# Two reorderings in a fused residual kernel: when the first chunk's part stores go out, and when the last weight rows are prepared

## The chip, the cores and the metric

The kernel runs on one core of one Trainium2 chip. The metric is the device time of one execution in microseconds. Before the change it is 2336.32 us, the median of 3 runs (2335.76 to 2338.26). The execution that was profiled took 2337.22 us.

## The reference

The input `x` has 32 sequences of 64 rows and 1024 columns in float32. Four layers are added to it in turn; each reads what the one before left:

```
x = x + causal_convolution(x, state-space parameters) * length_mask
x = x + einsum('bsi,boi->bso', x, W1[id1[b]])         # 16 matrices of 1024 x 1024
x = x + einsum('bij,bkj->bik', x, W2[id2[b]])         # 16 matrices of 1024 x 1024
gate = x @ W_gate.T + 0.5 * low_rank(A_gate, B_gate, id3[b])   # 2752 hidden units
up   = x @ W_up.T   + 0.5 * low_rank(A_up, B_up, id3[b])
act  = silu(gate) * up
x = x + act @ W_down.T + 0.5 * low_rank(A_down, B_down, id3[b])
```

The matrix of the second and third layer and the low-rank pair of the fourth are picked for each sequence.

## The kernel before

The 32 sequences are worked through in four chunks of 8, that is 512 rows each. The convolution is done for all at the start (about the first 200 us). Then the adapters of chunk 0 run. After that a loop over the chunks runs the gated layer, and the adapters of the next chunk are slotted into it, one at a time (`other()`, called by `between`): an adapter is 128 matmuls on TensorE (L297) over eight weight tiles of 512 KB, `wa`, which SyncE's queue loads (L167).

**The gated layer.** The 2752 hidden units are ten pairs of 128-row blocks and a rest. `gated` makes two such pairs a call, once for the gate and once for the up half; I call one of these a step, so chunk 0 has ten steps (five groups, `g` 0 and 1). All products are done by the scheme of Strassen and Winograd, which needs seven block products in place of eight, but wants sums and differences of the weight blocks. `sides` makes four of them on VectorE (L453 to L456).

- In chunk 0 (`halves`) the scheme is applied once. Each step has two units `m` = 0 and 1 of seven products (L540). While it holds the weights, it also makes and stores to DRAM what the later chunks will want: `kept(q)` makes a second level of sums in one of two `kept` buffers and stores it to `sums` (L517), and `kept_parts` stores some raw blocks and first-level sums to `parts` (L527 and L530). All these stores are issued by GpSimd (POOL).
- In the chunks 1 to 3 (`quarters`) the scheme is applied twice and the stored `sums` and `parts` are loaded.

In a step the sums come in the order `kept(0)`, `kept(1)` (unit 0), `kept(2)`, `kept(3)` (unit 1). The third needs the buffer of the first, so VectorE's L453 in it waits until the first store has landed. Behind it VectorE has L572 and L574, which read PSUM banks that TensorE's sixth product of the unit writes again. `kept_parts` is called just before `kept(2)`, but a store goes out when POOL's queue reaches it: POOL and SyncE are ordered by the planner, while TensorE, VectorE and ScalarE follow the program's order. `kept_parts` makes four stores a step: for `wts[0][1]` (256 KB) and `sts[0]` (768 KB), which are ready before unit 0, and for `wts[1][1]` (128 KB) and `sts[1]` (384 KB), ready during it.

The loaded weight tiles (`wf`, `wd`, `wa` and others) share nine rotating 512 KB buffers of `wpool`. A load into a buffer waits in SyncE's queue until all that read it is done, stores from it included, and all later loads wait behind it.

**The down product.** At the end of each of three blocks of hidden units, `ffn` multiplies the activations with `W_down` (L1018): for each of four `h`, over slices `s0` of the block, seven products `j`. In the last block there are two slices. With the second slice of each `h`, the tail products `po<-rest,wl` are added: `wl` holds the gathered low-rank rows (two gathers, POOL, L326) and the last 64 rows of `W_down`; `rest2` is their moving operand. `wl` needs a copy of 64 partitions on ScalarE (L1007) and one subtraction on VectorE (L1008). Only the tail of the last product, `j` = 2, reads the difference. `rest2` is written by `low_rank_down` on VectorE: a multiply (L410), an add (L412) and four copies (L416).

After the first slice the program calls `down_sides` (four `sides` operations for weights to come) and, at `h` = 0, `low_rank_down`.

Of the kernel before, what the change touches and what calls it, by code (L numbers as in the profile page):

```python
# [41 lines left out]
TQ, KQ = TH // 2, KH // 2  # L42
QP = KQ * P
# [30 lines left out]
def kernel(  # L74
# [25 lines left out]
    nc = tc.nc  # L100
# [12 lines left out]
    def ps_tile(name):  # L113
        return psum.tile([P, 512], F32, tag="ps", name=name)
# [266 lines left out]
    FIRST, SECOND = slice(0, P // 2), slice(P // 2, P)  # L381
# [115 lines left out]
    def halves(c, gi, g, o, xb, sides0, early, also=lambda: None):  # L497

        name = f"{c}_{gi}_{g}"
        lt, copy_lt = low_rank_of(c, gi, g)  # L500
        wts, sts, sides_of = ([x] for x in sides0)

        def kept(q):

            src = [
                [wts[m][0] for m in range(MG)],
                [wts[m][1] for m in range(MG)],
                [sts[m][:, 0:2] for m in range(MG)],
                [sts[m][:, 2:3] for m in range(MG)],
            ][q]  # L510
            n = 1 if q == 3 else 2
            t = qpool[0].tile([P, 2, 4, KQ, P], F32, tag="kept", name=f"kept{q}_{name}", bufs=2)
            a11, a12, a21, a22 = (
                src[m][:, :, k * KQ : (k + 1) * KQ, :] for m in range(MG) for k in range(2)
            )
            sides(a11, a12, a21, a22, *(t[:, :n, i] for i in range(4)))
            nc.gpsimd.dma_start(  # L517
                sums[2 * gi + g][2 * q : 2 * q + n].rearrange("j p e -> p j e"),
                t[:, :n].rearrange("p j i k f -> p j (i k f)"),
            )  # L520

        def kept_parts():

            d = parts[2 * gi + g]
            for lo, n, at_ in ((0, 1, [wts[m][1][:, 0:1] for m in range(MG)]), (1, 3, sts)):
                to = d[lo : lo + n].rearrange("j p e -> p j e")
                nc.gpsimd.dma_start(  # L527
                    to[:, :, : 2 * QP], at_[0][:, :n].rearrange("p j k f -> p j (k f)")
                )
                nc.gpsimd.dma_start(  # L530
                    to[:, :, 2 * QP :],
                    at_[1][:, :n, KQ:].rearrange("p j k f -> p j (k f)"),
                )

        for m in range(MG):
            ws = sides_of[m]

            def product(ps, j, start):
                for kt in range(KH):
                    nc.tensor.matmul(  # L540
                        ps,
                        ws[j][:, kt, :],
                        xb[j][:, kt, :],
                        start=start and kt == 0,
                        stop=kt == KH - 1,
                        skip_group_check=True,
                    )


            pa, pb, pc = (ps_tile(f"pf{i}_{name}_{m}")[:, :TH] for i in range(3))  # L550
            c11, c12, c21, c22 = (
                o[:, i, m, t * TH : (t + 1) * TH] for i in (0, 1) for t in (0, 1)
            )
            u, v = (
                gpool.tile([P, 2 * TQ], F32, tag=f"u{i}", name=f"u{i}_{name}_{m}", bufs=1)
                for i in range(2)
            )
            product(pa, 0, True)
            nc.scalar.copy(u, pa)
            product(pb, 5, True)  # L560
            nc.scalar.copy(v, pb)
            nc.vector.tensor_add(u, v, u)
            if m == 0:
                copy_lt()
                for at_, x in zip((wts, sts, sides_of), halves_sides(gi, g, 1)):
                    at_.append(x)
                also()
            else:
                kept_parts()
                kept(2)  # L570
            product(pc, 6, True)
            nc.vector.tensor_add(c22, pc, u)  # L572
            product(pb, 4, True)
            nc.vector.tensor_add(c22, pb, c22)  # L574
            kept(3 * m)
            product(pa, 1, False)
            nc.scalar.copy(c11, pa)
            product(pb, 2, False)
            nc.vector.tensor_add(c12, pb, u)
            if m == 0:  # L580
                kept(1)
            else:
                early()
            product(pc, 3, False)
            nc.vector.tensor_add(c21, pc, u)
            o_m = o[:, :, m]
            nc.vector.tensor_add(o_m, o_m, lt[:, :, m])
        if g == 0 or (gi + 1) * MG not in [m1 for _, m1 in BLOCKS]:
            return halves_sides(gi + g, 1 - g, 0)
# [274 lines left out]
    def ffn(c, xb, sides0, others):  # L864
# [40 lines left out]
        for block, (m0, m1) in enumerate(BLOCKS):  # L905
            last = m1 == FM
# [4 lines left out]
            def down_sides(done=False):  # L911
                nonlocal sides0
                if not todo:
                    if c == 0 and not last and sides0 is None and (done or block == 0):
                        sides0 = halves_sides(m1 // MG, 0, 0)
                    return
                h, s0 = todo.popleft()
                name = f"{c}_{block}_{h}_{s0}"
                wt = wpool.tile([P, 2, 2, SEG, P], F32, tag="w", name=f"wd_{name}")
                nc.sync.dma_start(  # L920
                    wt.rearrange("p i k s f -> p (i k s f)"), wd[h, s0 // SEG]
                )
                st = gpool.tile([P, 3, SEG, P], F32, tag="s", name=f"s_{name}")
                down[h, s0] = stationary([wt[:, 0], wt[:, 1]], SEG, st)
# [11 lines left out]
            for gi in groups:  # L936
                end = gi == groups[-1]
# [27 lines left out]
            if block == 0:  # L965

                wl = gpool.tile([P, KH, 3, P], F32, tag="cu", name=f"wm_{c}", bufs=1)
# [10 lines left out]
            if last:  # L978


                wl = gpool.tile([P, 2, 2, L // 2], F32, tag="lt", name=f"wl_{c}", bufs=1)
# [8 lines left out]
            for h in range(KH):  # L990
# [7 lines left out]
                for s0 in range(m0, m1, SEG):  # L998
                    end = s0 + SEG == m1
                    ws = down.pop((h, s0))  # L1000
                    tails = {}
                    if block == 0:
                        w = [wl[:, h, i] for i in range(3)]
                        tails = {1: (w[0], 0), 3: (w[1], 0), 4: (w[1], 1), 2: (w[2], 1)}
                    elif end and last:
                        if h == 0:
                            nc.scalar.copy(wl[SECOND, 1], wl[SECOND, 0])  # L1007
                            nc.vector.tensor_sub(wl[:, 1, 0], wl[:, 1, 0], wl[:, 1, 1])  # L1008
                        w = [[wl[:, t, i, h * P : (h + 1) * P] for i in (0, 1)] for t in (0, 1)]
                        tails = {1: (w[0][0], 0), 3: (w[0][1], 0), 4: (w[1][1], 1), 2: (w[1][0], 1)}  # L1010
                    for j in (0, 5, 6, 4, 1, 3, 2):
                        terms = [(ws[j][:, i, :], ab[s0 - m0 + i][j]) for i in range(SEG)]
                        if j in tails:
                            w, t = tails[j]
                            a = rest2[:, t] if last else rest1[:, t * TH : (t + 1) * TH]
                            terms.insert(SEG if s0 == m0 else 0, (w, a))
                        for i, term in enumerate(terms):
                            nc.tensor.matmul(  # L1018
                                pss[j],
                                *term,  # L1020
                                start=(s0 == m0 and i == 0 and home[j] % 2 == 0),
                                stop=(end and i == len(terms) - 1),
                                skip_group_check=True,
                            )
                    down_sides(h == KH - 1 and end)
                    if s0 == m0 and block == 1 and h < KH - 1:
                        other()
                    if h == 0 and s0 == m0:
                        tv = low_rank_down(at, ins, f"d{block}_{c}", tv, last)
                    if h == 1 and s0 == m0 and not last:  # L1030
                        at = next_at()
                    if s0 == m0 and last and h and more_come:

                        if h < KH - 1:
                            ready = raw.popleft()()
                        if h == 1:
                            raw.append(columns(au, c + 1, KT, f"u_{c + 1}"))
                        steps[h]()
# [497 lines left out]
```

## Time and profile before

| | us |
|---|---|
| median of 3 runs | 2336.32 |
| profiled execution | 2337.22 |
| its span, first to last instruction | 2335.6 |
| TensorE matmul, busy | 2256.3 (97%) |
| VectorE, busy | 1319.6 (57%) |
| ScalarE, busy | 379.7 (16%) |
| GpSimd, busy | 268.7 (12%) |
| moved by DMA | 684.96 MB, of it 82.37 MB in GpSimd's queue |

The granted TensorE clock was 0.998 over the span. The stretches that the change touches lie in this execution at about 349 to 840 us (the steps of chunk 0) and about 840 to 850, 1360 to 1370, 1880 to 1890 and 2280 to 2290 us (the first `h` of the last down product of each chunk). Share of busy time alone says little here, since TensorE is busy nearly throughout: what counts is where TensorE stands still, and for whom.

### The profile page before, as it was taken

To read this page: it belongs to the slowest core of one execution; us is meant where nothing else is said; L and a number is where in the kernel's file an instruction comes from. 1 tells how busy PE (TensorE), PEld (TensorE's weight loads), DVE (VectorE), ACT (ScalarE), POOL (GpSimd) and SP (SyncE) were. 2 spreads that over 40 slices of the span, in tenths; PEclk is the share of its full clock that TensorE was granted. 3 is DMA by queue.
4 is the path that set the end of the run, shared out by engine and by line. 5 is a ranking of instruction groups with operands and counts; after the bars stand their busy time and mean duration, and the time that the engine had idled before them with its cause. 6 is when DMAs were issued, how large, how long until landed. Compare 5 with 4: busy or idle time off the path is not lost.

```text
span 2335.6 us, 53669 instructions
## 1 busy us (share of the span) xinstructions
PE 2256.3 (97%) x21674; PEld 1863.4 (80%) x21674; DVE 1319.6 (57%) x2792; ACT 379.7 (16%) x822; POOL 268.7 (12%) x387
## 2 busy tenths in 40 slices
PE   5999889999999999999999999999999999999999
PEld 4996437677768789678768889688769889799997
DVE  7411116657636676646534677646535676577585
ACT  4200002010101112112102212112102212121220
POOL 3323002211101121000000011000000011100000
PEclk9999999999999999999999999999999999999999
DMA  8989998779997956889997956889997947285581
GB/s 293 366 314 361 407 409 304 279 293 345 357 365 290 348 202 209 309 291 344 366 349 291 359 188 229 308 297 360 358 347 284 359 159 266 95 292 204 193 278 62
DMA packets 201802, 684.96 MB, mean 293 GB/s; under 512 B 26178, under 2 KB 28482, under 8 KB 201042
## 3 DMA queue, kind: packets, MB, share of 16 engines
q1 hardware_dynamic: 169570, 590.50, 69.2%
q0 software_dynamic: 25184, 82.37, 9.4%
q10 hardware_dynamic: 6800, 8.65, 1.0%
q8 instruction: 171, 2.80, 0.5%
q14 instruction: 77, 0.63, 0.1%
HBM read 614.02 MB, written 67.40 MB: 292 GB/s over the span
## 4 chain that ended last, share of the span: by engine, by line
PE 77%; DMA 14%; issue 5%; DVE 3%; POOL 1%; ACT 0%; SPq 0%; POOLq 0%; ACTq 0%; DVEq 0%
PE pq L631 28%; PE po L1018 22%; PE pa L297 11%; DMA wa<-in_w 8%; PE pc L1324 5%; PE pr L764 4%; PE pf L540 3%; DMA sums<-kept 2%; PE pe L427 2%; DMA hk<-kp 1%; PE pl_d L398 1%; DMA wf<-in_wg 1%; DMA wa<-sums 1%; POOL parts L530 0%; DVE br L1126 0%
## 5 line engine op out<-in xcount | busy, mean ns | idle before, releaser
L297 PE MATMUL pa<-wa,x 128*32 128x256 f32 x7872 | 457.6, 381 | 26.2 <-DMA wa<-in_w 24.1
L297 PEld LDWEIGHTS pa<-wa,x 128*32 128x32 f32 x7872 | 243.0, 110 | 225.8 <-DMA wa<-in_w 63.8
L631 PE MATMUL pq<-xd,wa 128*128 128x128 f32 x3360 | 415.3, 275 | 0.3 <-DMA wa<-sums 0.2
L631 PEld LDWEIGHTS pq<-xd,wa 128*128 128x128 f32 x3360 | 394.8, 192 | 0.9 <-DMA wa<-sums 0.7
L631 PE MATMUL pq<-xd,wb 128*128 128x128 f32 x2520 | 323.9, 276 | 0.0
L631 PEld LDWEIGHTS pq<-xd,wb 128*128 128x128 f32 x2520 | 300.6, 192 | 3.8 <-DMA wb<-parts 0.2
L307 DVE STREAM_TRANSPOSE y<-pa 128x512 f32<-128x512 f32 x64 | 45.9, 717 | 291.8 <-PE pa L297 291.8
L1324 PE MATMUL pc<-uf,hk 128*128 128x256 f32 (+7 forms) x1024 | 156.4, 315 | 12.7 <-DMA hk<-kp 8.1
L1018 PE MATMUL po<-act,wd 128*128 128x256 f32 x640 | 168.6, 386 | 0.0
L1324 PEld LDWEIGHTS pc<-uf,hk 128*128 128x128 f32 x1024 | 150.8, 197 | 17.6 <-issue 11.7
L1018 PE MATMUL po<-actd,wd 128*128 128x256 f32 x640 | 164.2, 379 | 0.0
L1018 PE MATMUL po<-actd,s 128*128 128x256 f32 x640 | 164.2, 379 | 0.0
L326 POOL DMA_INDIRECT bgu<-in_bgu,rows x44 | 52.0, 1181 | 925.4 <-PE pe L427 822.1
L540 PE MATMUL pf<-xd,wf 128*128 128x256 f32 x640 | 150.6, 381 | 0.0
L1018 PEld LDWEIGHTS po<-act,wd 128*128 128x128 f32 x640 | 117.8, 190 | 30.0 <-issue 14.6
L453 DVE TENSOR_TENSOR s<-wd 128x256 f32<-128x256 f32 x80 | 33.9, 423 | 188.1 <-PE po L1018 188.0
L1018 PEld LDWEIGHTS po<-actd,wd 128*128 128x128 f32 x640 | 121.6, 190 | 16.5
L1018 PEld LDWEIGHTS po<-actd,s 128*128 128x128 f32 x640 | 121.6, 190 | 16.5
L540 PEld LDWEIGHTS pf<-xd,wf 128*128 128x128 f32 x640 | 120.9, 190 | 17.3
L540 PE MATMUL pf<-xd,s 128*128 128x256 f32 x480 | 116.1, 385 | 7.4 <-DVE up L574 3.6
L1046 ACT COPY uo<-po 128x256 f32<-128x256 f32 x48 | 17.9, 372 | 629.2 <-PE po L1018 627.1
L540 PEld LDWEIGHTS pf<-xd,s 128*128 128x128 f32 x480 | 91.4, 192 | 23.8 <-DVE up L574 5.5
(227 smaller groups left out, 2551.7 us busy)
## 6 DMA issues: line engine op xcount, KB each, us to landing
wa<-in_w SPq DMA_DIRECT2D x492, 512.0 KB, 7.3
wa<-sums SPq DMA_DIRECT2D x210, 512.0 KB, 5.9
wb<-parts SPq DMA_DIRECT2D x120, 384.0 KB, 5.4
wd<-in_wd SPq DMA_DIRECT2D x80, 512.0 KB, 7.0
wb<-in_wq SPq DMA_DIRECT2D x90, 384.0 KB, 5.7
hk<-kp SPq DMA_DIRECT2D x30, 1024.0 KB, 8.6
sums<-kept POOLq DMA_DIRECT2D x30, 1024.0 KB, 7.1
wf<-in_wg SPq DMA_DIRECT2D x20, 512.0 KB, 6.6
```

The costliest lines, as they stand in the source:

```text
L297: nc.tensor.matmul(acc[i * S : (i + 1) * S, s * 256 : (s + 1) * 256], xs[c][:, kt, lo + s * S : lo + (s + 1) * S], wt[:, i * 256 : (i + 1) ...
L307: nc.vector.transpose(y, acc)
L326: nc.gpsimd.indirect_dma_start(out=t, out_offset=None, in_=table, in_offset=bass.IndirectOffsetOnAxis(ap=at_, axis=0),)
L398: nc.tensor.matmul(ps[pair(j)], at[:, i, pair(j)], x_i[:, 2 * H * j : 2 * H * (j + 1)], start=(i == 0), stop=(i == n - 1),)
L427: nc.tensor.matmul(ps[:, at_ * 2 * H : (at_ + 1) * 2 * H], bt[pair(j), g], tms[table][pair(j)], start=(g == 0), stop=True, skip_group_chec ...
L453: nc.vector.tensor_add(s1, a21, a22)
L540: nc.tensor.matmul(ps, ws[j][:, kt, :], xb[j][:, kt, :], start=start and kt == 0, stop=kt == KH - 1, skip_group_check=True,)
L631: nc.tensor.matmul(ps[:, to * TQ : (to + 1) * TQ], w[i][:, k, :], xb[:, j, SLOT[i], k, :], start=start and k == 0 and to == 0, stop=k == K ...
L764: nc.tensor.matmul(ps, wts[i][:, kt, :], xs[c][:, kt, :], start=(kt == 0), stop=(kt == KT - 1),)
L1018: nc.tensor.matmul(pss[j], *term, start=(s0 == m0 and i == 0 and home[j] % 2 == 0), stop=(end and i == len(terms) - 1), skip_group_check=True,
L1046: nc.scalar.copy(u1, p1)
L1324: nc.tensor.matmul(ps[:, j, d * B :], hk[:, j, d * P : (d + 1) * P], uf[:, i + j, : KT - d, :].rearrange("p k b -> p (k b)"), start=(d == ...
```

## The change

It has two parts. In the first chunk, `kept_parts` ties its four stores behind the last store that `kept` made before it, that of `kept(1)`. In every chunk, the copy and the subtraction on `wl` move from the beginning of the second slice of `h` = 0 to the end of the first slice's products, ahead of `down_sides` and `low_rank_down`.

```diff
+        last_kept = []
         def kept(q):
...
-            nc.gpsimd.dma_start(
+            stored = nc.gpsimd.dma_start(
                 sums[2 * gi + g][2 * q : 2 * q + n].rearrange("j p e -> p j e"),
                 t[:, :n].rearrange("p j i k f -> p j (i k f)"),
             )
+            last_kept[:] = [stored.ins]
 
         def kept_parts():
 
             d = parts[2 * gi + g]
             for lo, n, at_ in ((0, 1, [wts[m][1][:, 0:1] for m in range(MG)]), (1, 3, sts)):
                 to = d[lo : lo + n].rearrange("j p e -> p j e")
-                nc.gpsimd.dma_start(
-                    to[:, :, : 2 * QP], at_[0][:, :n].rearrange("p j k f -> p j (k f)")
-                )
-                nc.gpsimd.dma_start(
-                    to[:, :, 2 * QP :],
-                    at_[1][:, :n, KQ:].rearrange("p j k f -> p j (k f)"),
-                )
+                with tc.issue_after(last_kept[0]):
+                    nc.gpsimd.dma_start(
+                        to[:, :, : 2 * QP],
+                        at_[0][:, :n].rearrange("p j k f -> p j (k f)"),
+                    )
+                    nc.gpsimd.dma_start(
+                        to[:, :, 2 * QP :],
+                        at_[1][:, :n, KQ:].rearrange("p j k f -> p j (k f)"),
+                    )
...
                     elif end and last:
-                        if h == 0:
-                            nc.scalar.copy(wl[SECOND, 1], wl[SECOND, 0])
-                            nc.vector.tensor_sub(wl[:, 1, 0], wl[:, 1, 0], wl[:, 1, 1])
...
+                    if last and h == 0 and not end:
+                        nc.scalar.copy(wl[SECOND, 1], wl[SECOND, 0])
+                        nc.vector.tensor_sub(wl[:, 1, 0], wl[:, 1, 0], wl[:, 1, 1])
                     down_sides(h == KH - 1 and end)
```

`issue_after` on the same queue is an order alone, with no semaphore. The program order that results: on TensorE and ScalarE nothing moves. On VectorE the subtraction stands eight instructions earlier in each chunk, behind the `sides` for the second slice of `h` = 0 and ahead of those for the first slice of `h` = 1. On POOL each step's order becomes gather of `bgu`, store of `kept(0)`, of `kept(1)`, the four stores of parts (first the two of `wts[m][1]`, then the two of `sts`), store of `kept(2)`, of `kept(3)`; before, the parts of unit 0 stood ahead of the gather and those of unit 1 behind it, ahead of `kept(0)`. On SyncE the order of the loads is the same.

## The prediction

> **What bounds the kernel now.** I read the page's busy times and its chain first: TensorE is the bound, and the chain leaves it only for transfers and a little VectorE work.
>
> ```profile
> PE 2256.3 (97%) x21674; PEld 1863.4 (80%) x21674; DVE 1319.6 (57%) x2792; ACT 379.7 (16%) x822; POOL 268.7 (12%) x387
> PE 77%; DMA 14%; issue 5%; DVE 3%; POOL 1%; ACT 0%; SPq 0%; POOLq 0%; ACTq 0%; DVEq 0%
> ```
>
> So an edit is worth what it does to TensorE's idle time. Second, who TensorE waited for from 339 to 875 us, the steps of chunk 0 (total, times, longest):
>
> ```profile
> PE pf L540 <- DVE up L574: 3.6, 3, 2.7
> PE pf L540 <- DVE act L574: 3.2, 2, 2.1
> PE pa L297 <- DMA wa<-in_w: 2.3, 6, 0.7
> PE po L1018 <- ACT at_g L373: 1.0, 1, 1.0
> ```
>
> The first two rows, 6.8 us together, are what the first edit can win. L574 is late because `kept(2)` ahead of it waits for a store; VectorE's waits in the same stretch have
>
> ```profile
> DVE kept L453 <- DMA sums<-kept: 21.6, 18, 3.4
> ```
>
> Third, one step in time, on POOL (start, duration, what), and the chain's row for the first of its `sums` stores (start, duration):
>
> ```profile
> 488.08 0.57 POOL L530 DMA_DIRECT2D parts<-wf  x1 [5.35 <-DVE wf L455]
> 488.68 0.76 POOL L530 DMA_DIRECT2D parts<-s  x1
> 492.08 0.73 POOL L517 DMA_DIRECT2D sums<-kept  x1 [2.63 <-DVE kept L456]
> 495.19 0.72 POOL L517 DMA_DIRECT2D sums<-kept  x1 [2.38 <-DVE kept L456]
> ```
> ```profile
> 492.08 6.75 DMA sums<-kept
> ```
>
> Half a megabyte of parts goes out less than 4 us ahead of the store on which VectorE will wait. Fourth, the second edit's place in chunk 0, VectorE and then TensorE:
>
> ```profile
> 843.10 0.42 DVE L456 TENSOR_TENSOR s<-wd,s 128x256 f32<-128x256 f32 x1
> 843.43 0.42 DVE L453 TENSOR_TENSOR s<-wd 128x256 f32<-128x256 f32 x1
> ...
> 845.62 0.91 DVE L416 COPY rest<-tv_d 32x128 f32<-32x128 f32 x4
> 846.55 0.69 DVE L1008 TENSOR_TENSOR wl<-wl 128x512 f32<-128x512 f32 x1
> ```
> ```profile
> 846.62 0.67 PE L1018 MATMUL po<-rest,wl 128*128 128x256 f32 x2 [1.05 <-ACT at_g L373]
> ```
>
> VectorE runs without a gap here, and TensorE stands still 1.05 us until the last copy of `rest` ends (845.62 + 0.91 = 846.53). The row names ScalarE, but its `wl` copy was over at 842.1; what ends last is L416. The other chunks show the same with idle times of 0.70, 0.69 and 0.69 us (at 1366.63, 1885.25, 2284.59).
>
> **Second edit: a loss.** The subtraction moves to between the two rows at 843.10 and 843.43. Where it stood, it cost nothing: the product that reads it, `j` = 2, starts its tail at 850.58, 3.3 us after it ended. In its new place it lies ahead of the copies that TensorE waits for, in a queue with no slack. Two independent 128x512 operations of VectorE start 0.60 us apart (L455 at 487.10, L456 at 487.70), so L416 ends 0.6 us later and TensorE waits 0.6 us more: 4 chunks x 0.6 = 2.4 us.
>
> It also meets a new wait: for the second gather of `wl`. That gather is issued at 839.11, 1353.58, 1872.20 and 2271.55 us and takes 5.0, 9.7, 9.6 and 10.3 us to land, that is 844.1, 1363.3, 1881.8 and 2281.8. The new slots are at 843.4, 1363.4, 1882.1 and 2281.4. So chunk 0 waits 0.7 us and chunk 3 0.4 us, with TensorE behind them. Bounds: nothing, if the gathers land a little earlier, to some 4 us, if those of chunk 0 fall behind the parts' bytes and the others take the longest landing. I take 1.1, the rows as they stand. Queued behind the waiting subtraction are the `sides` for the next `h`, L410, L412 and L416. Second edit: +2.4 + 1.1 = +3.5 us. The copy on ScalarE keeps its place and costs nothing.
>
> **First edit: what it can win.** A step's parts are 256 + 128 + 768 + 384 KB = 1.57 MB. POOL's queue moved 82.37 MB in 9.4% of the 16 engines' span, 0.375 MB/us when it runs. So the 0.52 MB of unit 1, less than 4 us ahead of `kept(0)`, are worth up to 1.4 us of its landing, and all four up to 4.2 us where loads still crowd the engines. TensorE's stalls behind L574 are, step by step, 2.69 (at 404.32), 0.13, 0.56, 1.12, 0.34, 0.09, 0.10 and 2.13 us (at 798.51). Six are below 1.4. At 786.25 the store of `kept(0)` took 8.69 us behind loads issued up to 774.4 that landed as late as 788.7, with 1.57 MB of parts among them; 2.13 us is less than what they took. At 404.32 POOL itself was late: `kept(0)` was ready at 391.2, but issued at 393.30, behind both pairs of parts; that order goes, and with it about 1.5 of the 2.69 us. I count the whole 6.8 us. Bounds: 6.8, and about 3 if half of the crowding is other loads. A rule of the Trainium skill, page "DMA: Bandwidth & Descriptors", section "Anatomy of one DMA — SWDGE (gpsimd) path", gives a transfer from GpSimd about 2.0 us and its bytes at 436 GB/s: an estimate of 4.4 us for `kept(0)`, where the trace has 6.75. By the rule 2.3 us a step could be won; by the rows 1.4. Both cover the six small stalls, so the sum is the same by either.
>
> **First edit: what it adds.** Four stores of 0.57, 0.57, 0.76 and 0.76 us move behind `kept(1)` on POOL: 495.2 + 0.7 + 2.7 = 498.6, before `kept(2)` is ready (501.5), so issuing costs nothing. But the reads of the weight buffers end later, and two who wait for that stand on the way.
>
> First, SyncE. In seven steps an adapter follows, and the loads of its `wa` 5 and 7 (counted from 0) go into the buffers that the two `wts[m][1]` held:
>
> ```profile
> 495.02 11.45 SPq L167 DMA_DIRECT2D wa<-in_w  x3
> ```
>
> These are `wa` 5 at 495.02, 6 at 502.28 and 7 at 506.14. Before, 5 went as soon as `kept(1)` had read the buffer. Now it waits until the part's store has landed, behind `kept(0)` and `kept(1)` in POOL's queue: `kept(1)` landed at 503.0; with less ahead of it I put it at 501.5, plus 0.39 MB at 0.375, so 502.5. Queued behind 5 are 6, 7 and all later loads. TensorE's adapter begins at 506.04 and uses a tile each 0.88 us: 5 at 510.4, 6 at 511.3, 7 at 512.2. Issued at 502.5 with the 5.8 us that `wa` 5 took among stores, it lands at 508.3. 6 follows it about 2 us later, at 510.3. 7 is issued, as before, when TensorE frees its buffer at 506.1, and before took 5.6 us (511.7), 0.5 us ahead of its use. Now two loads stand in front of it and 1.5 MB of `kept(2)` and `kept(3)`, pushed back by 1.15 MB of `sts`, run beside it. I estimate 6.5 us, 0.4 late: 7 x 0.4 = 2.8 us. Bounds: nothing, and 7 x 2.1 = 15 us, if each of the three loads moves at half of 0.375 MB/us (2.7 us each, from 503.5). The same page, section "Queues, rings and completion order", says that each engine takes turns between queues packet by packet, so the stores pushed back do not yield to the loads. By half of its 436 GB/s three loads from 503.5 and 2 us of fixed time end at 512.7, 0.5 us late: 3.5 us in place of 2.8, the sum +0.2 rather than -0.5.
>
> Second, VectorE writes `s` of unit 0 again for the next step (507.82), and now the store of `sts[0]` must have landed. It follows `kept(1)` with 1.18 MB in 3.1 us: 504.6 by the time above, 3 us ahead. Where no adapter lies between, after the first step, `kept(1)` landed at 376.40: 379.5 against 380.85. I count nothing; the bound is 2 us. The loads in the first two steps that also wait for these buffers (`cv`, `wr`, `wd`) are used 10 us or more later.
>
> **Sum.** -6.8 + 2.8 + 3.5 = -0.5 us on the profiled execution's 2337.22 us. That one stands 0.9 us above the median, which it leaves alone: 2336.32 - 0.5 = 2335.8 us.
>
> **Rivals.**
> - *The held buffers turn into a new wait* (slower). Once the loads of `wa` 5 to 7 come so late that the last lands more than 6.2 us after the adapter's first matmul, each of seven adapters pays. At 1.5 to 2.1 us each: -6.8 + (10.5 to 14.7) + 3.5, which is 2343.5 to 2347.7 us. From 0.47 us each on the change is a loss, from 1.15 us each on one of over 0.2%. For it: margins of 0 to 0.9 us in landings of 5.3 to 6.3 us. Against: 5 and 6 have 4 us between the part's landing and the adapter.
> - *The stalls go and nothing takes their place* (faster): the gathers in time, the loads as before: -6.8 + 2.4 = -4.4 us. The crowd of prefetches meets no parts, so that some of the 2.3 us of waits for `wa` go too: 2330.5 to 2331.9. For it: in the long run of loads after each adapter landings take 10 to 13 us beside the parts.
> - *The first half does not do what it says*: `kept(0)` is slowed by loads, not by parts, so `kept(2)` waits as before. Then 0 to -2, with up to 2.8, and +3.5: 2338 to 2340.6.
>
> **How the numbers follow.** My forecast 0.40, the third rival 0.14, the new wait 0.31, the faster one 0.15. A difference of 0.2% (4.7 us) is about what a measurement of this kernel can tell from no change. The first and third lie within it: with a small tail of theirs moved to slower, same 0.52, slower 0.33, faster 0.15. The forecast's own range is 2332 to 2340. The range for 8 in 10 leaves out the upper half of the slower rival and part of the faster one: 2331 to 2344.
>
> **What would show it.** Right: TensorE's waits on L574 fall from 6.8 us to under 1; the idle time before the first `po<-rest,wl` grows to about 2.4, 1.3, 1.3 and 1.7 us, with L1008 ahead of L410; SyncE's `wa` 5 is issued some 7 us later in each step; waits of `pa` for `wa` grow from 2.3 to about 5 us in chunk 0. Wrong: waits on `wa` beyond 10 us in chunk 0, or VectorE waiting at `s` L453 for the store of `sts[0]` with TensorE behind it; or L574's row unchanged.

## The result, and the profile after

The changed kernel takes 2357.48 us (median of 6 runs, 2350.36 to 2359.96); the kernel before, run beside it, 2336.04. The ratio is 1.0089, with a 95% interval of 1.0065 to 1.0113: about 21 us slower, where 2335.8 was predicted and 2344 was the upper end of the range. The profiled execution took 2359.26 us, its span is 2357.6. Lines have moved: L540 is now L545, L574 is L579, L517 is L519, L527 and L530 are L531 and L535, L1018 is L1020, L1008 is L1029.

The page's busy times say that no work was added; TensorE's share fell by a point. (That it is busy 5.5 us longer fits the half-clock stretches told of below.)

```profile
PE 2261.8 (96%) x21674; PEld 1861.9 (79%) x21674; DVE 1319.6 (56%) x2792; ACT 379.7 (16%) x822; POOL 267.9 (11%) x387
```

Who TensorE waited for in chunk 0, 339 to 900 us (total, times, longest):

```profile
PE pa L297 <- DMA wa<-in_w: 13.5, 12, 2.2
PE po L1020 <- DVE rest L416: 6.4, 1, 6.4
PE pf L545 <- DVE up L579: 1.4, 2, 0.9
PE pf L545 <- DVE act L579: 0.9, 1, 0.9
```

The stalls that the first edit was to win shrank from 6.8 to 2.3 us, so it does what it says. The waits for `wa` grew from 2.3 to 13.5, and the one ahead of the tail products from 1.05 to 6.4. VectorE in the same stretch: the waits of L453 for stores of `kept` fell from 21.6 us (18 times, ahead of `kept(2)` and of `kept(3)`) to 9.0 (9 times, all ahead of `kept(2)`), and a new wait is there.

```profile
DVE kept L453 <- DMA sums<-kept: 9.0, 9, 1.6
DVE wl L1029 <- DMA wl<-in_bd,rows_half: 4.7, 1, 4.7
```

One step on POOL (start, duration): both `kept` stores of unit 0 now go ahead of the four parts.

```profile
484.15 0.72 POOL L519 DMA_DIRECT2D sums<-kept  x1 [9.37 <-DVE kept L456]
487.26 0.73 POOL L519 DMA_DIRECT2D sums<-kept  x1 [2.38 <-DVE kept L456]
487.99 0.57 POOL L531 DMA_DIRECT2D parts<-wf  x1
...
489.86 0.77 POOL L535 DMA_DIRECT2D parts<-s  x1
493.80 0.72 POOL L519 DMA_DIRECT2D sums<-kept  x1 [3.17 <-DVE kept L456]
```

What that does to `wa` is best seen at the step whose adapter has the longest wait. SyncE's three loads `wa` 5 to 7, of before and then of after (start of the first issue, time to the end of the last):

```profile
595.18 11.66 SPq L167 DMA_DIRECT2D wa<-in_w  x3
```
```profile
599.59 4.31 SPq L167 DMA_DIRECT2D wa<-in_w  x3
```

The adapter begins at 606.41 us before and at 603.47 after. So the first load went out 11.2 us ahead of it, and now goes 3.9 us ahead; the other two keep about their places (the second 4.0 us ahead before and 3.3 after, the third 0.1 us behind the adapter's start in both), so that all three now go out within 4.3 us. TensorE in the changed kernel:

```profile
603.47 6.25 PE L297 MATMUL pa<-wa,x 128*32 128x256 f32 x112
611.95 1.24 PE L297 MATMUL pa<-wa,x 128*32 128x256 f32 x16 [2.23 <-DMA wa<-in_w]
```

Seven of the eight tiles run without a gap, and the last, `wa` 7, is 2.23 us late. Its row also shows a loss that is no wait: 16 matmuls take 1.24 us, where the other tiles take 0.89, since a stretch at half clock begins just after the stall. Windows of 3.41 us around it (stretch, its length, TensorE busy, granted clock, DMA share, GB/s):

```profile
609.31:612.72 3.41, 1.18 (x24) 1.00 1.04 422
612.72:616.13 3.41, 3.41 (x15) 0.50 1.02 416
```

Then the place of the second edit in chunk 0, VectorE and TensorE:

```profile
853.52 0.42 DVE L456 TENSOR_TENSOR s<-wd,s 128x256 f32<-128x256 f32 x1
858.62 0.69 DVE L1029 TENSOR_TENSOR wl<-wl 128x512 f32<-128x512 f32 x1 [4.68 <-DMA wl<-in_bd,rows_half]
859.23 0.42 DVE L453 TENSOR_TENSOR s<-wd 128x256 f32<-128x256 f32 x1
...
861.41 0.91 DVE L416 COPY rest<-tv_d 32x128 f32<-32x128 f32 x4
```
```profile
862.42 1.19 PE L1020 MATMUL po<-rest,wl 128*128 128x256 f32 x2 [6.42 <-DVE rest L416]
```

The subtraction waits 4.68 us for the gather, with the `sides` and the copies of `rest` queued behind it. The chain of waits has the gather as `849.53 9.00 DMA wl<-in_bd,rows_half`: issued at 849.53, landed at 858.53. Ahead of it in GpSimd's queue are the last step's `kept(2)` and `kept(3)`, pushed back by the parts. Landing times of `kept(3)`, chunk 0, median, before and then after:

```profile
sums<-kept POOLq DMA_DIRECT2D x10, 512.0 KB, 5.9
```
```profile
sums<-kept POOLq DMA_DIRECT2D x9, 512.0 KB, 11.0
```

In the chunks 1 to 3 the stall ahead of the tail products is 1.62, 2.22 and 1.89 us, before 0.70, 0.69 and 0.69.

**The sum of the profiled executions**, after less before: `wa` in chunk 0 +11.2, stalls behind L579 -4.5, tails +5.4 in chunk 0 and +3.65 in the others, all TensorE idle time taken together +16.6 (12.6 in chunk 0, 3.1 behind it, 0.9 ahead, where the kernels are alike); and half clock. Before, three stretches of 3.41 us ran at half clock, 10.2 us. After, seven such lengths, 23.9 us: one at 134.9, one at 612.7, two each at 814.1 and 858.5, one at 2305.7. Each takes up to 1.7 us of work away, so +6.9. Together 23.5, against 22.0 us between the spans; part of a half-clock stretch lies where TensorE stood still anyway.

### The profile page after: what moved, and what is told of

It is laid out like the page before. It is cut to its first block, busy times and chain, and to the rows that moved or that the text cites. A ratio compares the mean times of both kernels' runs of the same rounds, so it can differ in the third digit from the quotient of the medians.

```text
span 2357.6 us, 53653 instructions
## 1 busy us (share of the span) xinstructions
PE 2261.8 (96%) x21674; PEld 1861.9 (79%) x21674; DVE 1319.6 (56%) x2792; ACT 379.7 (16%) x822; POOL 267.9 (11%) x387
## 4 chain that ended last, share of the span: by engine, by line
PE 64%; issue 23%; DMA 7%; POOL 3%; DVE 1%; POOLq 1%; ACT 0%; SPq 0%; ACTq 0%; DVEq 0%
PE pq L636 28%; PE po L1020 19%; PE pa L297 7%; PE pc L1329 5%; PE pr L769 3%; DMA wa<-in_w 3%; DMA hk<-kp 2%; DMA wa<-sums 1%; PE pe L427 1%; POOL sums L519 1%; POOL bgu L326 1%; PE pl_d L398 1%; POOLq L360 1%; POOL parts L535 1%; DMA raw_d<-in_ad 0%
## 5 line engine op out<-in xcount | busy, mean ns | idle before, releaser
L1020 PE MATMUL po<-act,wd 128*128 128x256 f32 x640 | 170.3, 389 | 0.0
L1020 PE MATMUL po<-actd,s 128*128 128x256 f32 x640 | 166.3, 383 | 0.0
L1020 PE MATMUL po<-actd,wd 128*128 128x256 f32 x640 | 164.2, 379 | 0.0
L545 PE MATMUL pf<-xd,wf 128*128 128x256 f32 x640 | 151.8, 383 | 0.0
L453 DVE TENSOR_TENSOR s<-wd 128x256 f32<-128x256 f32 x80 | 33.9, 423 | 196.0 <-PE po L1020 195.8
L1020 PEld LDWEIGHTS po<-act,wd 128*128 128x128 f32 x640 | 118.9, 191 | 30.5 <-issue 14.8
L1020 PEld LDWEIGHTS po<-actd,s 128*128 128x128 f32 x640 | 123.0, 192 | 17.1
L545 PEld LDWEIGHTS pf<-xd,wf 128*128 128x128 f32 x640 | 121.7, 191 | 17.6 <-issue 0.2
L1020 PEld LDWEIGHTS po<-actd,wd 128*128 128x128 f32 x640 | 121.6, 190 | 16.5
L545 PE MATMUL pf<-xd,s 128*128 128x256 f32 x480 | 114.3, 381 | 3.1 <-DVE up L579 1.4
L545 PEld LDWEIGHTS pf<-xd,s 128*128 128x128 f32 x480 | 90.4, 190 | 18.6 <-DVE up L579 3.2
```

Source lines behind the costliest of these rows:

```text
L453: nc.vector.tensor_add(s1, a21, a22)
L545: nc.tensor.matmul(ps, ws[j][:, kt, :], xb[j][:, kt, :], start=start and kt == 0, stop=kt == KH - 1, skip_group_check=True,)
L1020: nc.tensor.matmul(pss[j], *term, start=(s0 == m0 and i == 0 and home[j] % 2 == 0), stop=(end and i == len(terms) - 1), skip_group_check=True,
```

## The experiments

My theory after the result: the tied stores cost the loads of `wa` their slack, by the held buffers and by the bytes that run beside them; the second edit costs what VectorE's order makes it cost, and meets a gather that the first made late; long stalls cost a second time through the clock. The rivals were that one of these does it all. The table gives every kernel's ratio to the kernel before, run beside it on the same chip, and the waits of its profile, one execution each, in chunk 0: for `wa`, behind L574 (both rows), and the stall ahead of the first tail product.

| kernel | ratio (95%) | wa | L574 | tail |
|---|---|---|---|---|
| before | 1 | 2.3 | 6.8 | 1.05 |
| the change | 1.0089 (1.0065 to 1.0113) | 13.5 | 2.3 | 6.42 |
| e14, the change again | 1.0076 (1.0052 to 1.0099) | 14.1 | 2.3 | 6.12 |
| e1, first edit alone | 1.0028 (1.0016 to 1.0040) | 16.6 | 2.8 | 1.05 |
| e15, the same again | 1.0040 (1.0023 to 1.0057) | 15.4 | 4.0 | 1.04 |
| e2, second edit alone | 1.0033 (1.0017 to 1.0049) | 4.2 | 4.2 | 3.34 |
| e16, the same again | 1.0031 (1.0016 to 1.0047) | 4.4 | 5.8 | 3.57 |
| e3, only `sts` tied | 1.0003 (0.9992 to 1.0014) | 5.6 | 4.2 | 1.05 |
| e4, only `wts` tied | 0.9997 (0.9984 to 1.0011) | 7.6 | 5.8 | 1.05 |
| e10, hold alone | 1.0014 (0.9998 to 1.0029) | 4.0 | 6.2 | 1.05 |
| e11, bytes alone | 1.0027 (1.0013 to 1.0042) | 9.8 | 5.3 | 1.04 |
| e9, change, last step untied | 1.0085 (1.0066 to 1.0104) | 17.6 | 1.4 | 3.34 |
| e5, rank first | 0.9989 (0.9976 to 1.0001) | 2.2 | 5.0 | 0 |
| e6, rank first, then the subtraction | 0.9978 (0.9962 to 0.9993) | 3.8 | 10.4 | 0 |
| e13, both edits, rank first | 1.0037 (1.0022 to 1.0051) | 14.5 | 1.6 | 2.11 |
| e7, e6 and first two steps tied | 0.9957 (0.9941 to 0.9972) | 1.6 | 1.4 | 0 |
| e12, e7 and the last step tied | 0.9967 (0.9949 to 0.9985) | 2.2 | 8.2 | 0.51 |

**The halves.** e1 is the first hunk of the diff alone, e2 the second.

> The first edit alone; the copy and the subtraction on wl stay where they were. Both theories (held buffers; bytes of the parts beside the loads) expect TensorE's waits for wa in chunk 0 as with both edits, 11 to 15 us, and those behind L574 at about 2 us. In chunk 0 the second gather of wl still lands late, so TensorE's idle time before the first tail product is 2 to 4 us, not 6.4. Chunks 1 to 3: 0.7 us each, as before. Time: 2336 + 11 - 4.5 + 2 = 2344 us, and 2 to 5 us more if the longer stalls draw half-clock stretches.

> The second edit alone. Chunk 0: the gather of wl lands about 5 us after its issue, as before the change, so the subtraction waits 0.7 us and TensorE's idle time there is about 2.4 us, not 6.4; chunks 1 to 3 between 1.3 and 2.3 us. Waits for wa and L574 in chunk 0 as before (2.3 and 6.8 us). Time: 2336 + 3.5 to 5 = 2339.5 to 2341 us. If the 6.4 us of chunk 0 were the second edit's own, it would show here too, with 2345 us.

Medians 2343.36 and 2341.3 us beside 2334.79: +8.6 and +6.5, by the ratios +6.5 and +7.7. In e1 the stall of 2 to 4 us that was expected ahead of the first tail product did not come; it stayed at 1.05: the gather landed at 863.33 us, 0.2 ahead of the subtraction in its old place, behind the copies of `rest`. In e2 the subtraction waits 1.5 us for the gather, and the four stalls ahead of the tail products are 3.34, 1.30, 1.30 and 1.73 us. The stall of 3.34 in chunk 0:

```profile
846.70 0.67 PE L1015 MATMUL po<-rest,wl 128*128 128x256 f32 x2 [3.34 <-issue]
```

and the clock behind it:

```profile
844.40:847.81 3.41, 1.11 (x5) 1.00 0.24 77
847.81:851.20 3.39, 3.39 (x9) 0.50 0.20 58
```

So in this execution the second edit is 4.5 us of stalls more than before and 1.7 us of clock. The halves came to some 14 us, the whole to 21. Whether that gap is real was tried later on one chip:

> The changed kernel itself, once more, for the comparison on one chip with its two halves. Theory (the two edits meet: the moved stores make the gather of chunk 0 late and with it the moved subtraction, and the long stalls bring half-clock slots): 19 to 22 us over before, 5 or more over the sum of the halves. Rival (the halves add up, and the 7 us between 14 and 21 came from other chips): as much over before as the two halves together, within 3 us.

> The first edit alone, once more: 6 to 9 us over before by the theory, more than 10 if the halves add up to the whole.

> The second edit alone, once more: 6 to 8 us over before by both (4.5 us of stalls, 3.34 of them in one place, and one or two half-clock slots).

Medians 2353.35, 2344.59 and 2344.85 us beside 2336.49: 16.9 against 8.1 + 8.4 = 16.5. The theory of a surplus fell; the halves add up, within intervals of some 5 us. That the gather is later in the whole (4.4 and 4.7 us of waiting against 1.5 and 1.8 in the second half alone) is seen in both pairs of profiles, but it is 3 us, and lies inside those intervals. In e16 the four stalls were 3.57, 1.71, 1.86 and 1.65 us, 5.7 more than before.

**Which of the tied stores?** Both kernels leave the subtraction in its old place.

```diff
 # e3; e4 has lo == 0
-                with tc.issue_after(last_kept[0]):
+                with tc.issue_after(last_kept[0]) if lo == 1 else ExitStack():
```

> Of the four part stores only those of sts (1.15 of 1.54 MB) are tied behind kept(1); those of the weight tiles go out early, and wl stays as before. Held buffers: the loads of wa 5 and 7 are free as before, so the waits for wa in chunk 0 fall back to 2 to 4 us, with L574 at 2 to 3: 2332 to 2335 us. Bytes beside the loads: most of the bytes that were moved are still moved, so the waits for wa stay at 8 us or more: 2341 to 2346 us.

> The other half: only the part stores of the weight tiles (0.38 MB) are tied behind kept(1), those of sts go out early, wl as before. Held buffers: SyncE's queue waits for these stores, so the waits for wa in chunk 0 stay at 8 to 13 us: 2340 to 2345 us. Bytes beside the loads: three quarters of the bytes are back where they were, so the waits for wa are 2 to 5 us: 2334 to 2338 us.

Medians 2335.5 and 2334.09 us beside 2334.79. Neither half of the first edit can be told from no change in time, while both together cost 6.5 to 9. In the traces each adds 3 to 5 us of waits for `wa`, and both together 11 to 15. So the waits lie between what the held buffers and what the bytes alone were expected to bring, in both kernels. To part the two causes cleanly, one kernel was made to hold the buffers with next to no bytes, and one to move the bytes with no hold.

```diff
 # e10: before, and
+            with tc.issue_after(last_kept[0]):
+                for m in range(MG):
+                    nc.gpsimd.dma_start(hold[2 * gi + g][m], wts[m][1][:, 0, 0, : P // 4])
```
```diff
 # e11: e3, and behind the tied stores of sts
+                        for m in range(MG):
+                            nc.gpsimd.dma_start(
+                                spare[2 * gi + g][m, :, : 2 * QP // (1 + m)],
+                                sts[m][:, 0, : KH // (1 + m)].rearrange("p k f -> p (k f)"),
+                            )
```

> The kernel before, all its stores in their places, and two more of 16 KB a step, of the two wts[m][1], tied behind the store of kept(1): they hold the buffers of wa 5 and 7 as long as the change does, but move next to no bytes. Theory (held buffers and bytes beside the loads each take a share of the loads' slack, and together more than the sum): wa 5 is issued some 4 to 5 us ahead of the adapter in place of 11, TensorE's waits on wa in chunk 0 come to 5 to 9 us, between the 2 to 4 us of the untied kernels and the 13 to 18 us of the tied ones; the time is 1 to 5 us over before (ratio 1.0005 to 1.002). Rival A (the hold does it all): 12 us or more, ratio 1.004. Rival B (the bytes do it all): under 4.5 us, ratio 1.000.

> The opposite: the two sts stores tied behind kept(1) as in the change, those of wts[m][1] in their old place, and beside them two more stores of as many bytes (256 and 128 KB, read from sts) behind kept(1). So the loads of wa 5 to 7 meet all the bytes that they meet in the change, and no buffer of theirs is held. Theory: TensorE's waits on wa in chunk 0 come to 5 to 9 us, the time 0 to 4 us over before. Rival A (the hold does it all): waits under 4.5 us, time as before. Rival B (the bytes do it all): waits of 12 us or more, ratio 1.003 or more.

Medians 2338.56 and 2340.22 us beside 2334.87. Waits of e10, then of e11:

```profile
PE pa L297 <- DMA wa<-in_w: 4.0, 6, 1.7
```
```profile
PE pa L297 <- DMA wa<-in_w: 9.8, 10, 2.5
```

By the ratios that is +3.3 us (interval -0.5 to +6.8) and +6.3 (3.0 to 9.8). In e10 SyncE's `wa` 5 was issued 3.8 to 4.4 us ahead of the adapter, nearly as late as in the change. Counted in the seven adapters of the steps alone, TensorE waited 3.7 us for `wa` in e10 and 8.3 in e11; the six profiled executions of kernels that tie nothing have 0.2 to 2.2, those with nine or ten steps tied 12.5 to 15.2. So the hold by itself brings some 1.5 to 3.5 us of waits more than these, and the 1.5 MB of stores that run beside the last loads bring 6 to 8 (e11 does add 3.9 MB in all to the kernel's traffic). In the change both meet, and `wa` 7 comes too late in all seven steps. How much of the time is the hold stays open: e10's time can't be told from no change, and its profiled execution was the fastest of twelve. Its waits came out below what the theory had and its time within it; in e11 both came out just above.

**The gather and the place of the subtraction.** e9 is the change with `if 2 * gi + g < 9 else ExitStack()` behind the tie. e5 and e6 alter the order on VectorE alone:

```diff
 # e5; e6 also has the copy and the subtraction on wl here, behind low_rank_down
+                    if h == 0 and s0 == m0 and last:
+                        tv = low_rank_down(at, ins, f"d{block}_{c}", tv, last)
                     down_sides(h == KH - 1 and end)
...
-                    if h == 0 and s0 == m0:
+                    if h == 0 and s0 == m0 and not last:
                         tv = low_rank_down(at, ins, f"d{block}_{c}", tv, last)
```

> The kernel before, with one order changed: at h = 0 of the last block low_rank_down stands ahead of down_sides on VectorE; the subtraction on wl keeps its old place. Theory (TensorE's stall ahead of the first po<-rest,wl is VectorE's queue: the four sides ahead of the copies of rest): the copies end about 1.4 us earlier, the stalls of 1.05, 0.70, 0.69 and 0.69 us go, the time falls by about 3.1 us (ratio 0.9987). Rival (what ends last is ScalarE's copy on wl or at_g, as the row of the profile names it): the stalls stay, the ratio is 1.000.

> As e5, and the second edit done in another place: copy and subtraction on wl behind low_rank_down, ahead of down_sides. Theory (in the change the subtraction costs because it stands ahead of the copies of rest; the place at the end of the first products is free in itself): no stall ahead of the first po<-rest,wl, the time of e5, some 3 us under before. Rival (the wait for the second gather is what costs, wherever the subtraction stands, since all that VectorE does next is behind it): VectorE's wait on wl comes back as waits of TensorE for s or xd in the next products, 1 to 4 us over e5.

> The changed kernel, with the stores of the last step of chunk 0 (the tenth) not tied. Theory (the gather of chunk 0 is late because the tied stores of that step push the stores of kept(2) and kept(3) back, right ahead of the gather; so the two edits cost more together than apart): VectorE's wait on wl in chunk 0 falls from 4.7 to 1.5 us or less, the stall ahead of the first po<-rest,wl from 6.42 to about 3.3 us; with one or two half-clock stretches less that is 3 to 6.5 us under the changed kernel, some 15 to 18 us over before (ratio 1.0064 to 1.0077). Rival (the gather is late by itself, as it was at times before): the wait stays at 4 to 5 us and the ratio at 1.0089.

> Both edits, all ten steps tied, but with low_rank_down ahead of the copy and subtraction on wl, and these ahead of down_sides. Theory (what the halves cost together beyond their sum lies in the stall ahead of the first po<-rest,wl): the first edit's cost less the 3.1 us of stalls that the order saves, 2 to 6 us over before; the gather may land late without harm. Rival (it lies in chunk 0's steps, in the loads of wa): 9 us or more over before.

e9: 2355.08 us beside 2334.2. The trace does what was expected, to the tenth:

```profile
DVE wl L1029 <- DMA wl<-in_bd,rows_half: 1.5, 1, 1.5
861.84 0.67 PE L1020 MATMUL po<-rest,wl 128*128 128x256 f32 x2 [3.34 <-issue]
```

The moved stores of the last step do make that gather late. But the ratio, 1.0085, hardly moved and missed the expected 1.0064 to 1.0077: 3 us are below what two such intervals can part, and this execution's waits for `wa` were the longest of all, 17.6 us.

e5 and e6: 2332.66 and 2329.06 us beside 2334.2. All four stalls ahead of the tail products are gone in both, and e6 is no slower than e5 (the 3.6 us between them are within the intervals; e5's own time can't be told from no change). So TensorE waited there for VectorE's queue, not for the copy on ScalarE that the row before named. And the subtraction costs nothing that shows at the end of the first products, if it stands behind `low_rank_down` and the gather is not late. What the second edit did wrong was to put it ahead.

e13: 2345.68 us beside 2336.49, 8.6 us by the ratio, more than the 2 to 6 expected and not less than the first edit alone (its interval, 5.1 to 11.9, parts neither the theory nor the rival). One row shows what came back:

```profile
856.20 1.10 PE L1020 MATMUL po<-rest,wl 128*128 128x256 f32 x2 [2.11 <-DMA wl<-in_bd,rows_half]
```

With VectorE out of the way TensorE waits for the late gather itself, 2.11 us, and a half-clock stretch follows. So in this execution the late gather takes about what the order saves (3.1 us): 2.11 of stall and up to 1.7 of clock. With the last step's stores tied, it costs in either order.

**The clock.** The change's stalls of 2.2 us had half-clock stretches behind them, that of before with 2.13 us at 798.51 had none. e8 lengthens four stalls by repeating L410:

```diff
-        nc.vector.tensor_mul(v, ps, bmask)
+        for _ in range({"0": 3, "1": 6, "2": 10, "3": 14}[name[-1]] if last else 1):
+            nc.vector.tensor_mul(v, ps, bmask)
```

> The kernel before, with VectorE's multiply L410 of the last block repeated 2, 5, 9 and 13 times more in the chunks 0 to 3, so that TensorE stands still about 1.65, 2.3, 3.6 and 4.9 us ahead of the first po<-rest,wl. Theory (the clock is halved for a slot of 3.41 us on a fixed grid whenever TensorE stood still for more than about half of the slot ahead of it): none behind the first stall; behind the second one only if it lies nearly whole in one slot; one behind the third if 1.8 us of it lie in one slot, one behind the fourth for sure; each costs 1.7 us beside its stall. Rival (only idle time longer than a whole window of 3.4 us brings the half clock, so the changed kernel's stretches at 612 and 814 us have another cause): none behind the first two, one or more behind the last two.

2354.51 us. The four stalls were 1.69, 2.75, 4.05 and 5.24 us. All half-clock stretches of one execution start on one grid of 3.41 us; in its slots, the windows around the second, third and fourth stall (columns as above):

```profile
1368.53:1371.94 3.41, 1.55 (x7) 1.00 0.31 88
1371.94:1375.35 3.41, 3.41 (x17) 1.00 0.19 58
1890.77:1894.18 3.41, 0.00 (x0) 1.00 0.25 72
1894.18:1897.59 3.41, 2.84 (x7) 0.50 0.26 65
2293.54:2296.95 3.41, 1.26 (x6) 1.00 0.05 20
2296.95:2300.36 3.41, 0.32 (x1) 0.50 0.00 0
2300.36:2303.78 3.42, 3.42 (x9) 0.50 0.00 0
```

The second stall, 2.75 us, was split by the grid: its larger piece left 1.86 us idle in one slot, and the clock stayed. In the slot from 2293.54 TensorE was busy for 1.26 us, and the next was halved. These four stalls alone would fit the rival too; what does not are the stalls of 2.23 us in the change and of 2.70 and 1.87 us at 402 and 534 us in e8, all shorter than a slot, each with a halved one behind. Counted over the slots of all profiled executions that show the grid (16 of 18), full-clock slots alone: with up to 1.7 us idle, 0 of some 10,500 were followed by a halved one; between 1.7 and 2.0 us, 16 of 33; above 2.0 us, 35 of 36. It is about half a slot of idle time in one slot, in one stall or several. At 814.1 in the change it was two, of 1.51 and 1.21 us.

**A version that beats both.** The first two steps have no adapter behind them, and in the six profiled executions that tie nothing the longest stall behind L574 (2.2 to 3.8 us) lies in the second. e7 is e6 with the four stores tied in these two steps alone, `free = 2 * gi + g in (0, 1)`; e12 has `(0, 1, 9)`.

> A version that should beat both: the order of low_rank_down ahead of copy and subtraction on wl ahead of down_sides, as measured, and the four stores tied only in the first two steps of chunk 0, where no adapter follows whose loads they hold. Theory: the stall at the second step (2.2 to 3.8 us at 401 to 404 us in the untied kernels, each time with a half-clock stretch of 1.7 us behind it) falls under 0.7 us; the rest is as in the version with the order alone: about 5 us under before in that, and 3 to 4 more here, 2326 to 2329 us (ratio 0.9965 to 0.9975). Rival (with the stall gone the next stalls in chunk 0 take its place): no more than 2 us from the version with the order alone.

> The same with the tenth step tied as well; no adapter follows it, but the gather of wl stands behind its stores on GpSimd's queue. Theory: the stall of 0 to 1.5 us in the last step goes, and the later gather (landing 3 us later) costs nothing, since nothing that TensorE soon needs is queued behind the subtraction any more: as the other or up to 1.5 us less. Rival (the gather late by 4 to 5 us holds VectorE's queue, and TensorE waits for the sums of h = 1): 1 to 3 us more than the other.

2325.56 and 2326.66 us beside 2334.87; e7 is 9 to 10 us faster than the kernel before (ratio 0.9957, 0.9941 to 0.9972). TensorE's waits in chunk 0 in e7:

```profile
PE pa L297 <- DMA wa<-in_w: 1.6, 2, 1.0
PE pf L546 <- DVE act L580: 1.0, 1, 1.0
PE pf L546 <- DVE up L580: 0.4, 1, 0.4
```

The stall in the second step and all tails are gone, and with them the half clock behind them. (The expectation has a half-clock stretch behind that stall each time; in e2 a stall of 2.25 us there had none.) How much of the gain is the order and how much the ties is not parted: e6, without the ties, had 5.1 us on another chip (1.6 to 8.9). Tying the last step too brings nothing that can be told (its tail waited 0.51 us for the gather). That the other steps' stalls were small in e7's profile is partly luck of that execution: in e12, tied alike there, they came to 8.2 us.

## Why the prediction was wrong, step by step

In the terms of the sum, -6.8 came as -4.5, +2.8 as +11.2 and +3.5 as +9.0, and half clock, which had no term, as up to +6.9.

- **The loads of `wa`: the term that failed most.** The working put 7 x 0.4 = 2.8 us and named 15 as the far bound; the profile has +11.2, or 12.3 in the seven adapters alone, 1.8 us each, and four other executions with all ten steps tied (e14, e13, e15, e1) have +11.8 to +14.3. The working's own sign of being wrong, waits for `wa` beyond 10 us, came. That its far bound was near is luck: by its own row, three loads of 2.7 us from 503.5 end at 511.6, ahead of the use at 512.2, and not 2.1 us late. The times of issue were right: `wa` 5 now goes 3.4 to 4.0 us ahead of the adapter, 502.5 against 506.04 in the working. The landings were too short: 5.9 to 8.1 us where it had 5.8, 8.1 to 10.0 for `wa` 6, which it let follow 2 us behind 5, and 7.4 to 9.4 for `wa` 7 where it had 6.5. Since 7 is wanted 6.0 us behind its issue, everything above that is paid at full price. The working took landings from a trace where 0.5 MB of parts went out near these loads, and used them where 1.5 MB do. The estimate worked out from the Trainium skill's page "DMA: Bandwidth & Descriptors", section "Queues, rings and completion order", 3.5 us, was as far off.
- **The rival "held buffers" had the price** (1.5 to 2.1 us each of seven) and a chance of 0.31, but the smaller part of its cause: alone, the hold brought 3.7 us of waits in the seven adapters (e10), the bytes 8.3 (e11). Its highest time, 2347.7, is below what was measured too, since the late gather and the clock are not in it.
- **What is won:** 4.5 us in the profile for 6.8. L574's stalls fell to 2.3, not under 1; the store of `kept(0)` is still slowed by loads. In six profiles with no step tied the two rows come to 7.3 us on average, in six with nine or ten tied to 2.4.
- **The subtraction: right in kind and, alone, in size.** The forecast tails of 2.4, 1.3, 1.3 and 1.7 us stand against 3.34, 1.30, 1.30 and 1.73 in e2 and 3.57, 1.71, 1.86 and 1.65 in e16. Its 2.4 + 1.1 = 3.5 us were 4.5 and 5.7 there, in e2 all of the difference in chunk 0. In the change VectorE waited 4.7 us for that gather: the working named this bound, up to 4 us "if those of chunk 0 fall behind the parts' bytes", and yet took the row as it stood. The first edit moves exactly those bytes; the two parts of one change were costed as though each were alone.
- **The clock was no term at all.** Every stall was priced at its own length. In the profile of before the stall of 2.69 us already had a half-clock stretch behind it, and the working had that stall on its list. Each execution's span times (1 - its mean granted clock) gives the time lost: on average 4.6 us over 114 executions of the kernel before, 9.2 over 12 of the change, 7.5 over 21 of the second edit alone, 5.2 over 18 of the first. (An upper figure, as above.) So some 4 to 5 us of the 17 to 21 are clock, and some 3 us for the second edit alone, of the order of what its time has over its stalls.
- **What was rightly left out:** in the profile after, VectorE never waits for the store of `sts[0]`, and no wait of TensorE is put down to issuing on POOL or to the copy on `wl`.
- **A slip that changed nothing:** the third rival's terms, 0 to -2, up to 2.8 and +3.5, reach 2342.6 us, not 2340.6.

The Trainium skill, page "TensorE: Matmul & The Clock Gate", section "Part 1: The HAM clock gate (the "warmup" mystery)", has the window: free-running, 3413 ns. The runs agree, 3.41 us on one grid. Its section "HAM oscillation — how this bites in real kernels" states the rule as no idle gaps above some 3.4 us; here 1.7 to 2.0 us of idle time in one window were enough in 16 of 33 cases and more than 2.0 us in 35 of 36, and the measurement decides.

## What to carry to other kernels

A store moved out of one crowd moves into another: before pricing it, list the transfers that run in its new place and how much slack each has, and give their landings the bytes that will then run beside them. Where two edits share a queue, cost the second with the first already made. And in an order written by hand, put ahead what the bottleneck waits for; with the stores in their old places the same subtraction cost 6 to 8 us in front of `low_rank_down` and nothing that could be told behind it.

## What the runs showed of the hardware

- TensorE's clock is halved for a slot of 3.41 us when it stood still for more than about half of the slot before (counts above), so a stall of 2 us can cost 3.7. Where a stall falls on the grid decides, and the grid lies differently in each execution: this makes up part of the spread between executions of one kernel. The twelve executions of the change had mean clocks of 0.994 to 0.998 and spans of 2348.3 to 2358.3 us; span times clock has a standard deviation of 2.0 us, where the spans have 3.7. In the kernel before, over 114 executions, it is 3.0 where the spans have 3.8; so most of its spread has other causes.
- The landing of a load of 512 KB depends on what runs beside it. The last load of the seven adapters took 5.3 to 6.3 us before, 6.1 to 7.8 with the two loads ahead of it bunched (e10), 6.3 to 8.6 with 1.5 MB of stores beside it (e11) and 7.4 to 9.4 with both; TensorE's waits there were 0.2, 3.7, 8.3 and 12.5 us.
- The second gather of `wl`, issued in the same queue behind the stores of `kept(2)` and `kept(3)`, landed 4.8 us after the last of them in the kernel before and 4.5 in the change: it took 5.0 us when these stores took 5.6 and 6.1 us, 9.0 when they took 10.45 and 10.81.
